# First modulation of an adaptive-norm block computed by channels, identity transposes ahead of it, and value products among the first keys

## The chip, the core and the metric

The kernel runs on one core of a Trainium2 chip. The metric is the device time of one execution in microseconds. The core's engines run side by side, each with its own queue of instructions in program order: TensorE (PE; its weight loads are listed apart as PEld), VectorE (DVE), ScalarE (ACT), GpSimd (POOL), and SyncE (SP), whose queue here issues the DMA transfers between device memory and on-chip memory. Engines wait for each other by semaphores.

## The reference

A transformer block with adaptive layer norm, in fp32: 4 batches of 512 tokens with 512 channels, 16 heads of 128, and a routed feed-forward layer of 8 experts. Cut to what matters here:

```python
mod = (_silu(L0_c) @ L0_wmod).reshape(4, 6, 1, 512)
sa, ca, ga, sb, cb, gb = (mod[:, 0], mod[:, 1], ..., mod[:, 5])
ga = (2 * (ga >= 0) - 1) * jnp.maximum(jnp.abs(ga), 0.25)      # gb likewise
h = _layernorm(x) * (1 + ca) + sa
x = x + ga * attention(h, Wq, bq, Wk, bk, Wv, bv, Wo, bo)      # causal, 16 heads
h = _layernorm(x) * (1 + cb) + sb
x = x + gb * ffn(h, ...)                                       # 2 of 8 experts, and shared ones
```

`sa` and `ca` are the shift and the scale of the first norm: 512 numbers for each of the 4 batches, from a 4x512 condition and 512x512 weights each. The change concerns how these two are made, and the order of the work around them.

## The kernel before

The order of the instructions on TensorE, VectorE, ScalarE and SP is written out by hand (`tc.manual_schedule`): each queue holds its instructions in the order in which the Python program creates them. GpSimd's queue keeps program order too. Generators split long pieces into steps, and `weave` places so many steps of one piece between so many of another.

**The opening.** SP issues the loads: the condition, the first batch's x (1 MB), the weights of the shift section `SA` (`wm`, 1 MB) and of the scale section `CA` (`wm2`, 1 MB), four small ones, and the first weights for keys, queries and values (`wk_t`, `wq_t`, `wv_t`; 512 KB each for `wk` and `wq`, 1 MB for `wv`). Each weight load is followed in `load_quadrants` by four additions on GpSimd (`sums_of_a`, lines 507 to 510). ScalarE makes `cs = silu(c)`.

- `modulation(sec, wm)`, line 169: `cs` is the small operand held in the array (4 columns), the 512 columns of the weights stream past it, four times for the four blocks of 128 inputs. The result is a 4x512 row in a bank of PSUM.
- `normed(0, 1)`: the layer norm's statistics and normalization of x, on VectorE.
- `modulate(sec, pm)`: VectorE copies the row (line 179) or adds one to it (line 177); for `SA` and `CA`, TensorE turns it by four small transposes (line 191), so that channels lie on partitions, and VectorE copies that into `mod` (line 194). For the other four sections the row is stored by a DMA.
- `quadrants(0)`: for each of four blocks of 128 channels, TensorE turns x (line 285), and ScalarE (even blocks, line 298) or VectorE (odd blocks, line 300) multiplies by the scale and adds the shift, into `h7`. Two buffers of PSUM alternate, so the third block's transposes wait for the first block's reader. Then `sums_of_b` makes three more sums and one in place on VectorE (lines 514 to 517): products are done in seven instead of eight quadrant products, and the sums are operands of them.
- `next_k(0, 0)`: seven products for the first two heads' keys, in the order 1, 2, 6, 7, 5, 4, 3 (`seven`). Products 1 and 2 read quadrants 0 and 2 of `h7`; 6, 7, 5 and 4 read the sums 5 and 4, the changed 1 and the sum 6; 3 reads quadrant 3. Each product has a buffer of PSUM out of three in rotation (tag `w`), freed by its readers on VectorE or ScalarE. Product 7's result goes through ScalarE to an addition on GpSimd (line 679), which the reader of product 4 on VectorE waits for.

**The query stretch.** `queries(0)` is 8 times seven products, 56 steps. Among them `weave` places 18 steps of `by_turns(next_v(0), rest_of_modulation())`: the seven value products (line 708) and the remaining four modulation sections, `GA`, `SB`, `CB`, `GB`, whose weights come one after the other into one buffer. For `GA` and `GB` VectorE makes six passes (lines 182 to 187). After this stretch come the attention of 16 heads with the other keys, values and output products woven in, the other batches, and the feed-forward layer.

Of the kernel before, what the change touches and what calls it, by code (L numbers as in the profile page):

```python
# [14 lines left out]
P = 128  # L15
B, S, D = 4, 512, 512
H, DH = 16, 128
NE, F, NSH = 8, 352, 2
NC = D // P
# [18 lines left out]
CAP = B * S  # L38
NT = TOPK * B * S // P + NE - 1
NA = NT - 3  # L40
NFILL = 15
NROW = NE * CAP + (NE - 1) * P
I32 = mybir.dt.int32
# [3 lines left out]
SA, CA, GA, SB, CB, GB = range(6)  # L47
# [3 lines left out]
def adaln_block_kernel(  # L51
# [18 lines left out]
    nc = tc.nc  # L70
# [10 lines left out]
    def bank(tag, name):  # L81
        if tag in ("ps", "pt"):
            return psum.tile([P, 512], F32, tag=tag, name=name)
        bufs = {"w": 3, "po": 1}[tag]
        return psum2.tile([P, 512], F32, tag=tag, bufs=bufs, name=name)

    ident = const.tile([P, P], F32, name="ident")
# [8 lines left out]
        out=before,  # L96
        in_=ones,
        compare_op=ALU.is_gt,
        fill=0.0,
# [31 lines left out]
    mod = const.tile([P, 2, NC, B], F32, name="mod")  # L131
# [23 lines left out]
    mod_rows = dram.tile([6, B, D], F32, name="mod_rows")  # L155
    cs = small.tile([P, NC, B], F32, tag="cs", bufs=1, name="cs")
# [9 lines left out]
    def modulation(sec, wm):  # L166
        pm = bank("ps", f"pm_{sec}")[:B, :]
        for c in range(NC):
            nc.tensor.matmul(
                pm, lhsT=cs[:, c, :], rhs=wm[:, c, :], start=(c == 0), stop=(c == NC - 1)  # L170
            )
        return pm

    def modulate(sec, pm):
        row = work.tile([B, D], F32, tag="gy", name=f"row_{sec}")
        if sec in (CA, CB):
            nc.vector.tensor_scalar_add(row, pm, 1.0)
        elif sec in (SA, SB):
            nc.vector.tensor_copy(row, pm)
        else:  # L180
            sgn = work.tile([B, D], F32, tag="gy", name=f"sgn_{sec}")
            nc.vector.tensor_scalar(sgn, pm, 0.0, 2.0, op0=ALU.is_ge, op1=ALU.mult)
            nc.vector.tensor_scalar_mul(row, pm, -1.0)
            nc.vector.tensor_max(row, row, pm)
            nc.vector.tensor_scalar_max(row, row, 0.25)
            nc.vector.tensor_scalar_add(sgn, sgn, -1.0)
            nc.vector.tensor_mul(row, row, sgn)
        if sec in (SA, CA):
            pt = bank("w", f"pmt_{sec}")
            for c in range(NC):  # L190
                nc.tensor.transpose(
                    pt[:, c * B : (c + 1) * B], row[:, c * P : (c + 1) * P], ident[:B, :B]
                )
            nc.vector.tensor_copy(
                mod[:, sec].rearrange("p c b -> p (c b)"), pt[:, : NC * B]
            )
        else:
            nc.sync.dma_start(out=mod_rows[sec], in_=row)

    def spread(dst, sec, b=None):  # L200

# [80 lines left out]
    def turned_block(b, n, xh, c):  # L282
        pt = bank("pt", f"pln_{n}_{b}_{c}")
        for t in range(NTB):
            nc.tensor.transpose(
                pt[:, t * P : (t + 1) * P], xh[:, t, c * P : (c + 1) * P], ident
            )
        return pt
# [223 lines left out]
    def sums_of_b(eng, w):  # L512

        eng.tensor_sub(w[:, 4], w[:, 3], w[:, 1])
        eng.tensor_add(w[:, 5], w[:, 4], w[:, 0])  # L515
        eng.tensor_sub(w[:, 1], w[:, 1], w[:, 0])
        eng.tensor_sub(w[:, 6], w[:, 5], w[:, 2])
# [76 lines left out]
    def load_wk(b, i):  # L594
        return load_quadrants("wk", wk, i, b)

    def load_wv(b, g):
        return load_quadrants("wv", wv, g, b, n=4 * DH, bufs=1)
# [257 lines left out]
    h7, late = {}, {}  # L856
# [28 lines left out]
    wm = load_wmod(att, "v", SA)  # L885
    wm2 = load_wmod(att, "wo", CA)
    for dst, src in ((bqT, bq), (bkT, bk), (bvT, bv), (gwT, router)):
        nc.sync.dma_start(out=dst, in_=src)
    wk_t = [load_wk(0, 0), load_wk(0, 1)]
    wq_t = [load_wq(0, 0), load_wq(0, 1)]  # L890
    wv_t = [load_wv(0, 0)]

    def quadrants(b, turned=()):
        h7[b] = att.tile([P, 7, 2, HW], F32, tag="h7", bufs=1, name=f"h7_{b}")
        for c in range(NC):
            turn(b, c, late["first"], h7[b], turned[c] if c < len(turned) else None)
            if c == NC - 1:
                sums_of_b(nc.vector, h7[b])
            else:
                yield  # L900

    NGB = B * NG
    kTs, vs, oSs, wos, qTs = {}, {}, {}, {}, {}

    def next_k(G, q):

        b, g = divmod(G, NG)
        kTs[G, q] = att.tile(
            [P, 2, S], F32, tag=f"kT{q}", bufs=2 - q, name=f"kT_{b}_{g}_{q}"
        )  # L910
        i = 2 * G + q
        w = wk_t.pop(0)
        save_sums("wk", i, b, w)
        yield from project_k(b, 2 * g + q, w, kTs[G, q])
        if i + 2 < 2 * NGB:
            wk_t.append(load_wk(*divmod(i + 2, H // 2)))
# [11 lines left out]
    def queries(b):  # L928
        return in_order(*(next_q(b, j) for j in range(H // 2)))

    def next_v(G):
        b, g = divmod(G, NG)
        vs[G] = att.tile([P, NTB, GH * DH], F32, tag="v", bufs=1, name=f"v_{G}")
        w = wv_t.pop(0)
        save_sums("wv", g, b, w)
        yield from project_v(b, g, w, vs[G])
        if G + 1 < NGB:
            wv_t.append(load_wv(*divmod(G + 1, NG)))
# [58 lines left out]
    def by_turns(*gens):  # L997

        gens = list(gens)
        while gens:  # L1000
            for gen in list(gens):
                if next(gen, gens) is gens:
                    gens.remove(gen)
                yield
# [13 lines left out]
    def weave(main, n, fill, count):  # L1018

        done = 0  # L1020
        for k in range(n):
            next(main, None)
            while done * n < count * (k + 1):
                done += 1
                next(fill, None)
# [11 lines left out]
    def drain(gen):  # L1037
        for _ in gen:
            pass

    SEVEN = 7

    def rest_of_modulation():
        secs = (GA, SB, CB, GB)
        wm = load_wmod(work, "xh", secs[0])
        for k, sec in enumerate(secs):
            yield
            yield
            modulate(sec, modulation(sec, wm))
            if k + 1 < len(secs):  # L1050
                wm = load_wmod(work, "xh", secs[k + 1])
# [22 lines left out]
    LAST = PLANS[:3] + [(0,) * 8]  # L1074

    with tc.manual_schedule(engines={ENG.PE, ENG.DVE, ENG.Activation, ENG.SP}):
        nc.scalar.activation(cs, cT, AF.Silu)
        load_lnexp()
        norm = normed(0, 1)
        pms = {SA: modulation(SA, wm), CA: modulation(CA, wm2)}  # L1080
        drain(norm)
        turned = [turned_block(0, 1, late[0], c) for c in range(2)]
        for sec in (SA, CA):
            modulate(sec, pms[sec])
        nc.vector.tensor_scalar_mul(sbk, bkT, qscale)
        nc.vector.tensor_sub(dbk, sbk[:, 1:H:2], sbk[:, 0:H:2])
        nc.vector.tensor_sub(dbq, bqT[:, H // 2 :], bqT[:, : H // 2])
        drain(quadrants(0, turned))
        drain(next_k(0, 0))
        fill = by_turns(next_v(0), rest_of_modulation())  # L1090
        weave(queries(0), 8 * SEVEN, fill, 18)
        drain(fill)

        pending, prepare = None, shared_sums()
        for G in range(NGB):
            b, g = divmod(G, NG)

            if G == 0:
                plans, fill = FIRST, in_order(next_k(G, 1), next_k(G + 1, 0))
            elif g == 0:  # L1100
                plans = OPENING
                fill = in_order(next_o(G - 1), next_k(G, 1), next_k(G + 1, 0))
            elif G == NGB - 1:
                plans, fill = LAST, in_order(next_k(G, 1), next_v(G), next_o(G - 1))
            else:
                plans = PLANS
                fill = in_order(
                    next_k(G, 1), next_v(G), next_o(G - 1), next_k(G + 1, 0)
                )
            for u in range(GH):  # L1110
# [25 lines left out]
                if (G, u) == (NGB - 1, 1):  # L1136
# [10 lines left out]
                        out=wst.rearrange("p c n -> p (c n)"),  # L1147
                        in_=wshr[:, NSC * SQ : NSC * SQ + NC * P],
# [21 lines left out]
                if G == 1 and u == 0:  # L1170
                    nc.sync.dma_start(
                        out=ys[NA * P :, :].rearrange("(p n) (c w) -> p (n c) w", p=P, w=P),
                        in_=nothing.unsqueeze(1).to_broadcast([P, (NT - NA) * NC, P]),
                    )

                k, n = GH * G + u - 1, NROW // P // NFILL
                if 0 <= k < NFILL:
                    nc.sync.dma_start(
                        out=xs[k * n * P : (k + 1) * n * P, :].rearrange(
                            "(p n) (c w) -> p (n c) w", p=P, w=P  # L1180
                        ),
                        in_=nothing.unsqueeze(1).to_broadcast([P, n * NC, P]),
# [253 lines left out]
    def other(i):  # L1436

        if i < 2 or i >= NA:
            return {}
# [146 lines left out]
    with tc.manual_schedule(engines={ENG.PE, ENG.DVE, ENG.Activation, ENG.SP}):  # L1586
# [39 lines left out]
        main, fill = shared(0), slots_found()  # L1626
# [15 lines left out]
        turned = {0: tile_in(0, xts.pop(0))}  # L1642
# [64 lines left out]
        main, fill = shared(2), combined()  # L1707
# [119 lines left out]
```

## Time and profile before

Three runs took 1762.41, 1763.12 and 1766.95 us; the median is 1763.12. The profiled execution took 1764.14 us, of which the span from the first to the last instruction is 1762.4.

| what | us |
|---|---|
| first matmul starts (waits for the shift section's weights) | 9.70 |
| x of the first batch in, statistics begin | 6.92 |
| scale and shift by channels both in `mod` | 22.35 |
| last block of the first norm turned | 25.82 |
| last of the four sums on VectorE ends | 32.33 |
| GpSimd through with the first loads' additions | 31.78 |
| first query product starts | 35.42 |
| first attention scores start | 115.59 |
| span ends | 1762.4 |

The DMA engines are busy from about 2 to 21 us with the opening's loads at close to 400 GB/s, and then idle until 36. In the timeline, each row gives the start and duration in microseconds, engine, line, operation, destination and sources, shapes, how many instructions are merged, and in brackets the idle time before it with what ended it. Rows of stages give for each engine the busy time and (in brackets) the number of instructions, in the order PE, PEld, DVE, ACT, POOL, then the granted clock of TensorE, the share of the DMA engines that was busy, and GB/s.

### The profile page before, as it was taken

What the parts mean: (1) busy time and instruction counts of PE and PEld (TensorE: products, weight loads), DVE (VectorE), ACT (ScalarE), POOL (GpSimd) and SP (SyncE); (2) the same over time, 40 slices, a digit from 0 to 9 for tenths busy, and PEclk for the clock granted to TensorE, in tenths of its full rate; (3) what the DMA queues carried; (4) which work ended last, traced back from release to release, by engine and by line L of the source; (5) the groups of instructions that cost most, each with busy time, mean ns of one, the idle gap of its engine ahead of it and who ended that gap; (6) DMA issues with size and microseconds to landing.
All of it is one profiled execution on the core that took longest, in us unless ns stands there. A gap on an engine that the chain in (4) does not pass through costs nothing. (4 is left out here: it accounts for less than half of the span.)

```text
span 1762.4 us, 21698 instructions
## 1 busy us (share of the span) xinstructions
PE 1701.7 (97%) x7550; PEld 1302.2 (74%) x7550; DVE 896.5 (51%) x1891; ACT 528.5 (30%) x1298; POOL 589.5 (33%) x703
## 2 busy tenths in 40 slices
PE   6999999999999999999999989999999999999998
PEld 4767787787778888688788867787788565655687
DVE  4454454546545455754655475444776232121298
ACT  1025444303453420444441144444320111111120
POOL 6335553314354220525330255533620111000370
PEclk9999999999999999999999999999999999999999
DMA  5569989736343254334324275615324555565352
GB/s 219 184 213 303 281 291 301 261 116 239 94 166 112 84 168 146 124 108 142 110 101 146 96 253 180 196 55 227 126 94 169 215 191 170 193 215 186 110 182 68
DMA packets 158526, 301.14 MB, mean 171 GB/s; under 512 B 19136, under 2 KB 99008, under 8 KB 151760
## 3 DMA queue, kind: packets, MB, share of 16 engines
q1 hardware_dynamic: 153296, 282.96, 47.7%
q0 software_dynamic: 5120, 16.78, 2.9%
q8 instruction: 61, 1.00, 0.2%
q14 instruction: 49, 0.40, 0.1%
HBM read 247.25 MB, written 97.03 MB: 195 GB/s over the span
## 5 line engine op out<-in xcount | busy, mean ns | idle before, releaser
L808 ACT ACTIVATE prob<-ps,nmax 128x128 f32<-128x128 f32 (+3 forms) x256 | 134.4, 525 | 363.2 <-DVE nmax L806 355.6
L660 PE MATMUL w_k<-h,wk 128*128 128x256 f32 x896 | 223.5, 387 | 4.6 <-DVE h L515 2.4
L745 PE MATMUL w_o<-wo,oS 128*128 128x256 f32 x896 | 208.9, 379 | 0.0
L708 PE MATMUL w_v<-wv,h 128*128 128x256 f32 x896 | 206.0, 379 | 1.3 <-DVE u_q L642 1.3
L622 PE MATMUL w_q<-h,wq 128*128 128x256 f32 x896 | 201.9, 380 | 1.8 <-DVE qT L648 1.8
L622 PEld LDWEIGHTS w_q<-h,wq 128*128 128x128 f32 x896 | 168.7, 190 | 27.8 <-issue 3.4
L660 PEld LDWEIGHTS w_k<-h,wk 128*128 128x128 f32 x896 | 165.9, 195 | 27.9 <-ACT p_k L672 5.3
L708 PEld LDWEIGHTS w_v<-wv,h 128*128 128x128 f32 x896 | 167.4, 190 | 22.9 <-DVE u_q L642 1.7
L745 PEld LDWEIGHTS w_o<-wo,oS 128*128 128x128 f32 x896 | 164.6, 190 | 21.3 <-issue 1.4
L797 PE MATMUL ps<-kT,qT 128*128 128x128 f32 (+3 forms) x512 | 173.2, 440 | 1.4 <-ACT prob L808 1.4
L839 PE MATMUL po<-probT,v 128*128 128x512 f32 (+3 forms) x512 | 150.4, 435 | 12.3 <-DVE probT L833 12.3
L839 PEld LDWEIGHTS po<-probT,v 128*128 128x128 f32 x512 | 95.5, 190 | 68.7 <-issue 30.3
L815 ACT ACTIVATE prob<-prob,rsum 128x128 f32<-128x128 f32 (+3 forms) x256 | 122.8, 551 | 63.2 <-DVE rsum L812 61.5
L825 PEld LDWEIGHTS ppt<-ident,prob 128*128 128x128 f32 x640 | 83.3, 143 | 73.4 <-issue 34.7
L758 POOL TENSOR_TENSOR xres<-xres,p_o 128x512 f32<-128x512 f32 x48 | 61.4, 1281 | 209.4 <-DVE xres L758 118.1
L806 DVE TENSOR_REDUCE nmax<-ps 128x1 f32<-128x128 f32 (+3 forms) x256 | 125.7, 491 | 8.8
L1259 PE MATMUL w_s<-h2s,ws 128*128 128x256 f32 x560 | 124.4, 381 | 3.3 <-DVE hid L1245 1.8
L1259 PEld LDWEIGHTS w_s<-h2s,ws 128*128 128x128 f32 x560 | 105.0, 190 | 20.8 <-issue 2.7
L825 PE MATMUL ppt<-ident,prob 128*128 128x128 f32 x640 | 108.4, 278 | 7.6 <-ACT prob L815 5.1
L804 DVE TENSOR_TENSOR ps<-ps,cmask 128x128 f32<-128x128 f32 x256 | 75.1, 293 | 60.4 <-PE ps L797 52.2
L1516 PE MATMUL pyt<-wdn,hTt 128*128 128x512 f32 (+1 forms) x216 | 98.7, 593 | 0.0
L1499 DVE TENSOR_TENSOR ht<-tsg,put 128x352 f32<-128x352 f32 x36 | 18.8, 521 | 147.5 <-PE put L1489 123.0
(281 smaller groups left out, 2348.9 us busy)
## 6 DMA issues: line engine op xcount, KB each, us to landing
wgu<-in_wexp_dram SPq DMA_DIRECT2D x36, 1408.0 KB
xs<-nothing SPq DMA_DIRECT2D x15, 2304.0 KB
wdn<-in_wexp_dram SPq DMA_DIRECT2D x36, 768.0 KB
wo<-sums_o SPq DMA_DIRECT2D x12, 1536.0 KB
wq<-sums_q SPq DMA_DIRECT2D x24, 640.0 KB
wk<-sums_k SPq DMA_DIRECT2D x24, 640.0 KB
wv<-sums_v SPq DMA_DIRECT2D x12, 1280.0 KB
xt<-xs SPq DMA_DIRECT2D x36, 256.0 KB
```

Source lines behind the costliest of these rows:

```text
L622: nc.tensor.matmul(dst, lhsT=w[:, sa, c, :], rhs=h7[b][:, sb_, c, :], start=c == 0, stop=c == 1,)
L660: nc.tensor.matmul(dst, lhsT=w[:, sa, c, :], rhs=h7[b][:, sb_, c, :], start=c == 0, stop=c == 1,)
L708: nc.tensor.matmul(dst[:, t2 * HW : (t2 + 1) * HW], lhsT=h7[b][:, sb_, c, t2 * P : (t2 + 1) * P], rhs=w[:, sa, c, :], start=t2 == 0 and c ...
L745: nc.tensor.matmul(dst[:, t2 * HW : (t2 + 1) * HW], lhsT=oSs[hp][:, sa, t2 * P : (t2 + 1) * P], rhs=w[:, hp, sb_, :], start=t2 == 0 and hp ...
L797: nc.tensor.matmul(ps[:, :n], lhsT=qT[:, q0 : q0 + P], rhs=kT[:, u % 2, :n], start=True, stop=True,)
L806: nc.vector.tensor_reduce(nmax, ps[:, :n], AX.X, ALU.max, negate=True)
L808: nc.scalar.activation(blk, ps[:, :n], AF.Exp, bias=nmax, accum_out=rsum[:, i : i + 1])
L815: nc.scalar.mul(blk, blk, rsum[:, k : k + 1])
L825: nc.tensor.transpose(pt[:, at : at + P], prob[:, QO[i] + j * P : QO[i] + (j + 1) * P], ident,)
L839: nc.tensor.matmul(po[:, j * P :], lhsT=v()[:, j, u * DH : (u + 1) * DH], rhs=probT[:, KO[j] : KO[j] + (NTB - j) * P], start=(j == 0), sto ...
L1259: nc.tensor.matmul(dst[:, n * HW : (n + 1) * HW], lhsT=ws[k][:, sa, c, :], rhs=h2s[b + n][:, sb_, c, :], start=(n == 0 and c == 0), stop=( ...
L1516: nc.tensor.matmul(py, lhsT=hT_t[:fn, k, :], rhs=wdn[i % 2][:fn, k * D : (k + 1) * D], start=(k == 0), stop=(k == len(FCH) - 1),)
```

## The change

Four edits.

1. `modulation_by_channels` takes the place of `modulation` and `modulate` for `SA` and `CA`. The weights are now what is held in the array, 128x128 at a time, and the 4 columns of `cs` stream past: 16 products a section, whose result has channels on partitions at once. One pass of VectorE moves it into `mod`.
2. `NIDLE = 48` transposes of the identity by itself are placed at the head of TensorE's queue; nothing reads their result.
3. The opening's order: statistics, shift section, transposes of two blocks, scale section, then `quadrants(0)` directly. The three passes that prepare biases (`sbk`, `dbk`, `dbq`) move behind it.
4. The four sums of the first batch are written out between the first products, and the first two value products are issued behind the first two key products. To that end the loads' order becomes keys, values, queries, queries, second keys; the query stretch has 16 filling steps left instead of 18.

```diff
+NIDLE = 48
...
+    def modulation_by_channels(sec, wm):
+        pm = bank("ps", f"pmt_{sec}")[:, : NC * B]
+        for k in range(NC):
+            for c in range(NC):
+                nc.tensor.matmul(
+                    pm[:, k * B : (k + 1) * B],
+                    lhsT=wm[:, c, k * P : (k + 1) * P],
+                    rhs=cs[:, c, :],
+                    start=(k == 0 and c == 0),
+                    stop=(k == NC - 1 and c == NC - 1),
+                )
+        dst = mod[:, sec].rearrange("p c b -> p (c b)")
+        if sec == CA:
+            nc.vector.tensor_scalar_add(dst, pm, 1.0)
+        else:
+            nc.vector.tensor_copy(dst, pm)
...
     def modulate(sec, pm):
...
-        if sec in (SA, CA):
-            pt = bank("w", f"pmt_{sec}")
-            for c in range(NC):
-                nc.tensor.transpose(
-                    pt[:, c * B : (c + 1) * B], row[:, c * P : (c + 1) * P], ident[:B, :B]
-                )
-            nc.vector.tensor_copy(
-                mod[:, sec].rearrange("p c b -> p (c b)"), pt[:, : NC * B]
-            )
-        else:
-            nc.sync.dma_start(out=mod_rows[sec], in_=row)
+        nc.sync.dma_start(out=mod_rows[sec], in_=row)
...
-    wk_t = [load_wk(0, 0), load_wk(0, 1)]
-    wq_t = [load_wq(0, 0), load_wq(0, 1)]
+    wk_t = [load_wk(0, 0)]
     wv_t = [load_wv(0, 0)]
+    wq_t = [load_wq(0, 0), load_wq(0, 1)]
+    wk_t.append(load_wk(0, 1))
...
     def quadrants(b, turned=()):
...
+        if b == 0:
+            return
+        sums_of_b(nc.vector, h7[b])
...
+        idle = bank("po", "idle")[:, :P]
+        for _ in range(NIDLE):
+            nc.tensor.transpose(idle, ident, ident)
         nc.scalar.activation(cs, cT, AF.Silu)
         load_lnexp()
         norm = normed(0, 1)
-        pms = {SA: modulation(SA, wm), CA: modulation(CA, wm2)}
         drain(norm)
+        modulation_by_channels(SA, wm)
         turned = [turned_block(0, 1, late[0], c) for c in range(2)]
-        for sec in (SA, CA):
-            modulate(sec, pms[sec])
+        modulation_by_channels(CA, wm2)
+        drain(quadrants(0, turned))
         nc.vector.tensor_scalar_mul(sbk, bkT, qscale)
+        keys, values, h = next_k(0, 0), next_v(0), h7[0]
+        next(keys)
+        nc.vector.tensor_sub(h[:, 4], h[:, 3], h[:, 1])
+        nc.vector.tensor_add(h[:, 5], h[:, 4], h[:, 0])
+        next(keys)
+        next(values)
+        nc.vector.tensor_sub(h[:, 1], h[:, 1], h[:, 0])
+        nc.vector.tensor_sub(h[:, 6], h[:, 5], h[:, 2])
         nc.vector.tensor_sub(dbk, sbk[:, 1:H:2], sbk[:, 0:H:2])
         nc.vector.tensor_sub(dbq, bqT[:, H // 2 :], bqT[:, : H // 2])
-        drain(quadrants(0, turned))
-        drain(next_k(0, 0))
-        fill = by_turns(next_v(0), rest_of_modulation())
-        weave(queries(0), 8 * SEVEN, fill, 18)
+        next(values)
+        drain(keys)
+        fill = by_turns(values, rest_of_modulation())
+        weave(queries(0), 8 * SEVEN, fill, 16)
         drain(fill)
```

More of the change, by code (lines that the diff above doesn't have):

```diff
@@ L172, in modulation @@
         return pm
+    def modulation_by_channels(sec, wm):
[14 more added lines that the diff above has]
+            nc.vector.tensor_copy(dst, pm)
     def modulate(sec, pm):
         row = work.tile([B, D], F32, tag="gy", name=f"row_{sec}")
-        if sec in (CA, CB):
+        if sec == CB:
             nc.vector.tensor_scalar_add(row, pm, 1.0)
-        elif sec in (SA, SB):
+        elif sec == SB:
             nc.vector.tensor_copy(row, pm)
@@ L888, in adaln_block_kernel @@
         nc.sync.dma_start(out=dst, in_=src)
-    wk_t = [load_wk(0, 0), load_wk(0, 1)]
+    wk_t = [load_wk(0, 0)]
+    wv_t = [load_wv(0, 0)]
     wq_t = [load_wq(0, 0), load_wq(0, 1)]
-    wv_t = [load_wv(0, 0)]
+    wk_t.append(load_wk(0, 1))
     def quadrants(b, turned=()):
@@ L896, in quadrants @@
             turn(b, c, late["first"], h7[b], turned[c] if c < len(turned) else None)
-            if c == NC - 1:
-                sums_of_b(nc.vector, h7[b])
-            else:
+            if c < NC - 1:
                 yield
+        if b == 0:
+            return
+        sums_of_b(nc.vector, h7[b])
     NGB = B * NG
```

## The prediction, made before the changed kernel was run

> **What bounds the kernel now.** I read the page from the top: the engines' shares, then the span in 40 slices.
>
> ```profile
> PE 1701.7 (97%) x7550; PEld 1302.2 (74%) x7550; DVE 896.5 (51%) x1891; ACT 528.5 (30%) x1298; POOL 589.5 (33%) x703
> PE   6999999999999999999999989999999999999998
> ```
>
> TensorE is busy in 97% of the span and only the first slice (44 us) falls below 8 tenths. Its idle time is 60.7 us, and the table of stages puts 9.7 us of it before the first matmul (9.70) and 4.8 us between that and 35.42, where the first query product starts. From 35.42 to 120 it idles 4.2 us. So the start is a chain of waits, and what follows is a TensorE queue: if the start ends earlier, all that follows moves. The change touches the start, so I read its timeline (start, duration, engine, line, operation):
>
> ```profile
> 9.70 9.83 PE L169 MATMUL pm<-wm,cs 128*4 128x512 f32 x16 [9.70 <-DMA wm<-in_wmod_dram]
> 19.46 1.09 PE L285 MATMUL pln<-ident,xh 128*128 128x128 f32 x8
> 21.02 0.67 DVE L177 TENSOR_SCALAR row<-pm 4x512 f32<-4x512 f32 x1
> 22.18 0.17 DVE L194 COPY mod<-pmt 128x16 f32<-128x16 f32 x1 [0.50 <-PE pmt L191]
> ...
> 25.93 1.39 DVE L514 TENSOR_TENSOR h<-h 128x512 f32<-128x512 f32 x1
> 27.36 1.63 DVE L515 TENSOR_TENSOR h<-h 128x512 f32<-128x512 f32 x1
> ...
> 29.14 6.44 PE L660 MATMUL w_k<-h,wk 128*128 128x256 f32 x20 [2.44 <-DVE h L515]
> 30.07 1.71 POOL L510 TENSOR_TENSOR wv<-wv 128x512 f32<-128x512 f32 x1
> 30.58 1.75 DVE L517 TENSOR_TENSOR h<-h 128x512 f32<-128x512 f32 x1
> ...
> 32.26 0.41 DVE L675 SCALAR_TENSOR_TENSOR kT<-w_k,p_k 128x256 f32<-128x256 f32 x1
> ```
>
> To be seen: the modulation's matmuls wait for their weights until 9.70 and take until 19.4; its scale reaches the channels at 22.35, through a row, four transposes and a copy on VectorE, twice; VectorE's four sums of the norm's blocks end at 32.33; and the second key product's sum (32.26 to 32.67) stands behind all four. The fifth key product needs its buffer, so it starts at 32.7, and the keys end at 35.42.
>
> **TensorE's clock.** Rows of stages with the granted clock (the column after the engines):
>
> ```profile
> 22.20:25.61 3.41, 1.92 (x12) 1.64 (x13) 2.56 (x6) 1.56 (x2) 3.33 (x6) 1.00 0.00 0
> 25.61:29.03 3.42, 1.09 (x6) 0.61 (x4) 3.27 (x4) 0.47 (x1) 3.34 (x3) 1.00 0.00 0
> 29.03:32.44 3.41, 3.30 (x8) 2.52 (x8) 3.41 (x3) 0.00 (x0) 2.75 (x2) 0.50 0.00 0
> 1035.95:1039.37 3.42, 1.70 (x10) 1.12 (x10) 3.32 (x7) 0.93 (x4) 2.79 (x3) 1.00 0.57 204
> 1039.37:1042.78 3.41, 3.41 (x10) 2.42 (x10) 1.41 (x4) 1.96 (x7) 3.33 (x6) 0.50 0.47 156
> ```
>
> The clock halves for whole stretches of 3.41 us on one grid (29.03, 1032.54 and 1039.37 are all steps of it). It halves after a stretch with 1.70 us of TensorE work or less and stays after one with 1.92. The first modulation matmuls are slow too, though the record says 1.00: weight loads come every 0.85 us from 10.51, and every 0.43 from 15.50.
>
> **The change, part by part.**
>
> *48 turns of the identity.* It is ready at 1.5 us. Full speed is 0.107 us a turn (the eight transposes' weight loads: 0.85 us), half speed 0.213. Half speed lasts for the rest of a stretch and one full stretch, 3.4 to 6.8 us, so they end at 1.6 + 3.4 + 32 x 0.107 = 8.4 to 1.6 + 6.8 + 16 x 0.107 = 10.1. Weights land at 9.66; nothing else is queued on TensorE. Here a rule speaks against the change: the Trainium skill, "TensorE: Matmul & The Clock Gate", Part 4, says of transposes that the full clock "doesn't engage for transpose-mode (it doesn't count as PE-busy the same way)". By that rule the 48 end at 1.6 + 10.2 = 11.8, 2.1 us after the weights, and warm nothing. The rows above disagree: of the 1.92 us in 22.20 to 25.61, 1.29 are transposes, and without them 0.63 would be less than the 1.70 that lost the clock. I take the row; the rule stays as a rival.
>
> *Modulation by channels.* Removed: two row passes (0.68, 0.67), 8 transposes, two copies, and 16 streams of 512 columns (9.8 us, 6.9 had they been at 0.43). Added: 16 products a section, each two instructions as all fp32 products here, with 128x128 weights for 4 columns. The nearest row is the router's, 8 such instructions with 8 columns:
>
> ```profile
> 449.12 0.96 PE L323 MATMUL prt<-gwT,hT 128*128 128x8 f32 x8
> 449.93 1.10 PE L797 MATMUL ps<-kT,qT 128*128 128x512 f32 x2
> ```
>
> They occupy 449.12 to 449.93: 0.102 us each, so 32 take 3.3 us. Shift section 9.70 to 13.0; two blocks' transposes (x is normed by 12.85) 0.86, to 13.85; scale section to 17.15 (its weights: the queue's next issue at 12.5 waited for them); 0.25 until VectorE sees it, 0.17 for its pass: **the scale is there at 17.55 instead of 22.35.** Nothing shows whether weight loads with 4 columns hold the clock. Bounds: 0.102 and, at half clock, 0.204. I take 0.102, as the router's row was measured at full clock; the other end is a rival.
>
> *Norm, sums and first products.* ScalarE and VectorE turn two blocks at once (0.8 each; before, three bias passes, 22.27 to 23.47, stood ahead of VectorE's): 17.6 to 18.4; two blocks transposed (0.66 and 0.44 more), the last turned by 20.35. The bias pass of 0.45, then the sums from 20.85 instead of 25.93. They are slow beside GpSimd: line 515 takes 0.69 in the other three batches and 1.63 here, alternating with GpSimd's wv additions (1.6 a pair). The changed order puts wv's additions second, until about 22.4, and the smaller ones (0.72) after. So 1.6 for the first sum and 0.6 + 0.7 = 1.3 for the others: 22.4, 23.7, key sum 24.1, 25.4, 26.7, then bias differences (0.8), value sum (0.7) 28.2, next key sum 28.6. TensorE meanwhile: keys 1 and 2 to 21.3, values 1 and 2 (1.73 each, wv lands about 16.7, behind wk at 14.0) to 24.7, keys 6 and 7 to 26.5; key 5 needs the buffer that the value sum frees: 28.2, keys done 30.8, query 1 to 31.7.
>
> *GpSimd's queue.* The second key weights' additions are now last of the loads', and the keys' own GpSimd sum (line 679) stands behind them. GpSimd has been solid from 14.09: 16 small additions at 0.69 and 4 of 1.27 are 16.2, plus some 2.1 for turns lost to VectorE: 32.4 (it was 31.78). Then 0.72 for that sum and 0.42 for VectorE's key sum, which frees the buffer of the next value product: this starts at 33.5, ends at 35.2. **That wait takes the place of the one removed**; without it the product would start at 31.7.
>
> Compare equal work. At 35.2 the keys, query 1 and three value products are done. Before: 35.42 + 0.86 + 3 x 1.73 = 41.4. **Gain 6.2 us.**
>
> *The query stretch.* Fill steps now come every 3.5 main steps (56/16; it was 56/18). Gates' six VectorE passes (58.14 to 61.7) stop TensorE for 1.29 and 1.81 us; in the new order the blocking reader is the second behind them, not the first: +0.45 and +0.3. The last weights' wait (1.14: landing 5.4 after issue) recurs twice, seven products (6.0) against 1.1 + 5.4 = 6.5: 2 x 0.5, -0.1. Together **+0.7**. On SP the store of wv's sums moves ahead of the next key load, but that load waits for the keys' last product anyway: nothing.
>
> Sum: -6.2 + 0.7 = -5.5. The profiled execution took 1764.1 (span 1762.4): 1758.6. The shown runs' median lies 1.0 lower; I take half of that: **1758.1**.
>
> **Rivals.**
>
> 1. *More.* GpSimd is through at 31.2 (pairs cost it less), and the query stretch loses nothing: 1764.1 - 7.2 = 1757, on the same half 1756.5. For it: bounds of +0.7 to nothing. Against it: solid GpSimd rows.
> 2. *Half the warmth.* Either the turns don't warm (end 11.8, shift section 5.8 us, scale at 22.1), or the small products let the clock fall (one stretch at half rate: scale at about 20, four early products half slow). Both leave the value products in the old hole, 3.5, less the query stretch: -2.9, **1761**. For it: the cited rule; small products are nearly all weight loads. Against it: the 1.92 row.
> 3. *Slower: cold array throughout the opening.* Neither turns nor small products count. Turns end at 11.8, sections take 6.5 each, the transposes 1.7: scale at 26.8, +4.4; blocks 0.9 slower; the first four products another 2.6 at half clock, while the sums run free of GpSimd by then. The value product that ended at 41.4 ends at 45.9, with the query stretch +5.2: **1769.3**. It decides if the first full clock comes after 15 us.
>
> **How the numbers follow.** Forecast 0.52, more 0.19, half 0.17, slower 0.12. Range: the forecast's own is 1756.5 to 1760 (GpSimd 1 us either way, query stretch 0.7); with rivals 1 and 2 it becomes 1755.5 to 1765, and leaves out the slower one. This kernel tells 0.3%, 5.3 us, from no change, nearly the forecast itself; its own spread falls 0.31 beyond, 0.21 within. Faster 0.31 + 0.19 = 0.50; same 0.21 + 0.17 = 0.38; slower 0.12.
>
> **What would show it.** The first modulation product at 9.7 with instructions every 0.10 us; channel scale before 18; sums from about 21, at 1.3 for the last three; GpSimd's line 679 sum beginning at 32 or later with TensorE idle before the third value product; clock of 1.00 until 30. Wrong, if small products come every 0.2 us, the first wait on TensorE is not the weights, or the stretch from 42 to 116 grows by over 2 us.

## The result, and the profile after

The changed kernel is slower. Nine runs took 1768.37 to 1772.94 us, median 1770.36; nine runs of the kernel before, on the same chip, 1761.06 to 1766.95, median 1762.54. The ratio is 1.0045, with a 95% interval of 1.0036 to 1.0053. The forecast was 1758.1, and its range ended at 1765.

The profiled execution took 1770.12 us, its span is 1767.2, against 1764.14 and 1762.4 before. From the page of the changed kernel, the busy time of the engines and TensorE's row of slices:

```profile
PE 1711.9 (97%) x7638; PEld 1320.8 (75%) x7638; DVE 893.8 (51%) x1889; ACT 527.6 (30%) x1298; POOL 587.6 (33%) x703
PE   9999999999999999899999999999899999999998
```

The first slice rose from 6 to 9 tenths, as was meant. The 24th, which had 8, has 9 now, and the 17th has 8 instead: such digits flip at nine tenths, and the two cancel. The 29th (about 1237 to 1281 us) fell to 8 without a counterpart. It is far from the opening, and there the time was lost. To find it I laid the starts of the same work side by side:

| start of | before, us | after, us | difference |
|---|---|---|---|
| first attention scores | 115.59 | 111.50 | -4.1 |
| last output product of the attention | 1240.4 | 1236.0 | -4.4 |
| first product with the shared experts' sums (tile `pst`) | 1240.6 | 1245.0 | +4.4 |
| first product of the routed experts' gates (tile `pgt`) | 1354.2 | 1360.9 | +6.7 |
| last product of all | 1757.2 | 1762.0 | +4.8 |

So in these two profiles the opening did gain, by 4.1 us, and the gain was kept for 1100 us. Then 8.8 us go between two neighbouring pieces of work, and 2.3 more just behind. TensorE's waits in the changed kernel (what waited, for what, us in total, times, longest) have a row that the kernel before has not:

```profile
PE pst L1254 <- DMA h2s<-h: 8.6, 1, 8.6
```

`h2s` is the second norm's result, which the feed-forward layer reads back from device memory. In the timeline of the kernel before, its load is issued on SP at 1221.13, 19.5 us ahead of its first reader:

```profile
1219.78 1.02 PE L797 MATMUL ps<-kT,qT 128*128 128x512 f32 x2
...
1221.13 0.96 SPq L1205 DMA_DIRECT2D h2s<-h  x2
...
1240.64 7.03 PE L1231 MATMUL pst<-h2s,wst 128*128 128x512 f32 x16
```

In the changed kernel it is issued at 1240.12, behind the last additions of the last output product:

```profile
1238.84 1.26 POOL L766 TENSOR_TENSOR xres<-xres,u_o 128x512 f32<-128x512 f32 x1
1240.12 0.80 SPq L1228 DMA_DIRECT2D h2s<-h  x2
...
1245.04 9.54 PE L1254 MATMUL pst<-h2s,wst 128*128 128x512 f32 x16 [8.64 <-DMA h2s<-h]
```

And the waits of SP's queue say what this one transfer stood for (a row each for what came last):

```profile
SPq L1228 <- DVE u_o L787: 15.4, 1, 15.4
SPq L1228 <- POOL xres L766: 6.5, 1, 6.5
SPq L1228 <- ACT p_o L788: 1.6, 1, 1.6
```

All three waits are for work on the output product's temporaries (`p_o` and `u_o` are written on ScalarE and VectorE, and GpSimd's addition into `xres` reads them). As data these have nothing to do with `h2s`. A load that waits for tiles it doesn't use waits for their place. The addresses in the built programs, in bytes of a partition, show the overlap:

```
                        before and e1_place       after and e2_before_moved
h2s_0                       93248 .. 107584         93248 .. 107584
p1, u2, u3, p5 (512 wide)  133184 .. 141376        100416 .. 108608
qT                          100416 .. 133184        108608 .. 141376
```

The pool gives places by the first appearance of a name. Before, `qT` (opened by `queries(0)`) appeared ahead of the four 512-wide temporaries of value and output products. In the changed kernel `next_v(0)` starts first, so the temporaries took the place under the later `h2s_0`. The last reader of `qT`, the scores shown above, ends at 1220.80, just ahead of the load at 1221.13; the temporaries are in use until the last output product.

The price is the idle time, 8.64 us, and a halved clock behind it. A row of stages of the changed kernel shows the clock (PE, PEld, DVE, ACT, POOL, then the granted clock):

```profile
1245.00:1248.00 3.00, 2.96 (x4) 1.44 (x5) 0.59 (x1) 0.00 (x0) 2.84 (x3) 0.50 1.07 456
```

The 16 products that took 7.03 us took 9.54, 2.5 more. Together that is 11.1 us.

**The opening after**, from the timeline (TensorE, VectorE and GpSimd rows that answer to those shown of before):

```profile
1.56 8.34 PE L1090 MATMUL idle<-ident 128*128 128x128 f32 x48 [1.56 <-POOL ident masks.py:199]
...
10.20 3.71 PE L179 MATMUL pmt<-cs,wm 128*128 128x4 f32 x32 [0.30 <-DMA wm<-in_wmod_dram]
...
13.76 1.42 PE L293 MATMUL pln<-ident,xh 128*128 128x128 f32 x8
...
14.98 6.83 PE L179 MATMUL pmt<-cs,wm 128*128 128x4 f32 x32
...
21.84 0.17 DVE L188 TENSOR_SCALAR mod<-pmt 128x16 f32<-128x16 f32 x1 [7.73 <-PE pmt L179]
...
25.91 0.68 DVE L1103 TENSOR_TENSOR h<-h 128x512 f32<-128x512 f32 x1
...
28.03 3.62 PE L716 MATMUL w_v<-wv,h 128*128 128x256 f32 x16
...
31.48 4.48 PE L668 MATMUL w_k<-h,wk 128*128 128x256 f32 x20
...
33.96 0.72 POOL L687 TENSOR_TENSOR u_k<-u_k,u_k 128x256 f32<-128x256 f32 x1 [1.33 <-ACT u_k L680]
...
36.66 1.89 PE L716 MATMUL w_v<-wv,h 128*128 128x256 f32 x8
```

The shift section took 3.71 us, the scale section, the same 32 instructions, 6.83. Why is in the rows of stages (columns as before, the clock behind the engines):

```profile
10.93:14.34 3.41, 3.41 (x32) 3.41 (x32) 2.09 (x5) 0.07 (x1) 0.00 (x0) 1.00 1.11 381
14.34:17.76 3.42, 3.42 (x19) 3.42 (x18) 0.00 (x0) 0.00 (x0) 3.15 (x5) 0.50 0.99 400
17.76:21.17 3.41, 3.41 (x17) 3.41 (x18) 0.00 (x0) 0.00 (x0) 3.33 (x4) 0.50 1.00 402
21.17:24.58 3.41, 2.33 (x11) 2.25 (x12) 0.98 (x2) 1.32 (x2) 3.33 (x6) 0.50 0.50 206
24.58:27.99 3.41, 3.41 (x10) 2.76 (x9) 2.80 (x4) 0.71 (x2) 3.33 (x5) 0.50 0.47 195
```

By the record TensorE was busy for the whole of the first stretch, with products of 4 columns for most of it, and the clock halved all the same. It stayed halved for four stretches. So the scale was in `mod` at 22.01, only 0.3 us earlier than before (22.35), and the sums begin where they did (25.91). What the opening gained is the two value products in the old hole: at 35.80 the keys are done, 0.38 later than before, but 2 x 1.73 us of value products are done as well. That is 3.1 us, and the query stretch gave 1.0 more.

### The profile page after: what moved, and what is told of

Read it like the earlier page. It is cut to its first block, busy times and chain, and to the rows that moved or that the text cites. A ratio compares the mean times of both kernels' runs of the same rounds, so it can differ in the third digit from the quotient of the medians.

```text
span 1767.2 us, 21870 instructions
## 1 busy us (share of the span) xinstructions
PE 1711.9 (97%) x7638; PEld 1320.8 (75%) x7638; DVE 893.8 (51%) x1889; ACT 527.6 (30%) x1298; POOL 587.6 (33%) x703
```

## The experiments

My theory after the result: the place of the buffers costs some 11 us, the opening is worth some 5, and the opening was held down first by the clock in the scale section. The rivals: the late load is a mere consequence of something else in the order (then claiming `qT` earlier changes nothing); or the opening gained nothing that the end can see. All ratios are against the kernel before on the same chip.

| kernel | median, us | ratio | 95% interval |
|---|---|---|---|
| after | 1770.36 | 1.0045 | 1.0036 to 1.0053 |
| e1_place | 1759.45 | 0.9971 | 0.9959 to 0.9982 |
| e2_before_moved | 1772.54 | 1.0049 | 1.0035 to 1.0062 |
| e3_wide | 1758.24 | 0.9964 | 0.9950 to 0.9977 |
| e4_no_turns | 1762.73 | 0.9994 | 0.9986 to 1.0003 |
| e5_late_wk | 1756.61 | 0.9964 | 0.9953 to 0.9975 |
| e8_bias_early | 1756.58 | 0.9961 | 0.9946 to 0.9976 |
| e6_values_only | 1759.06 | 0.9977 | 0.9969 to 0.9985 |
| e7_turns_only | 1762.34 | 0.9996 | 0.9987 to 1.0004 |
| e9_first_key | 1752.67 | 0.9946 | 0.9931 to 0.9960 |
| e10_no_turns | 1756.46 | 0.9961 | 0.9947 to 0.9974 |

The medians of the kernel before beside these were 1764.27 (e1 to e4), 1762.77 (e5 to e8) and 1763.1 (e9, e10).

### The place: given back to the changed kernel, taken from the kernel before

e1_place is the changed kernel with `qT` claimed ahead of the first value product. No instruction is changed.

```diff
+    def open_q(b):
+        qTs[b] = att.tile([P, H * S], F32, tag="qT", bufs=1, name=f"qT_{b}")
+
     def next_q(b, j):
-        if j == 0:
-            qTs[b] = att.tile([P, H * S], F32, tag="qT", bufs=1, name=f"qT_{b}")
+        if j == 0 and b not in qTs:
+            open_q(b)
...
         next(keys)
+        open_q(0)
```

> The changed kernel, with only the place of one buffer put back: the query tile is claimed before the value products claim their four temporaries, so on-chip addresses are those of before. Theory 'place': in the changed kernel the feed-forward stage's first input (h2s) lies over the temporaries of the last output product, so its load waits for that product's readers, TensorE idles 8.6 us and runs its first matmuls at half clock (9.54 instead of 7.03). Put back, both go: the load is issued near 1217, no idle before the matmuls pst, and the time falls by about 11 us, from 1770.4 to 1759 (1758 to 1761). Rival 'something else late there': the wait moves to another transfer of that stage and less than 3 us come back, 1767 to 1770.

e2_before_moved is the opposite: the kernel before, with the four temporaries claimed ahead of `qT`.

```diff
         drain(next_k(0, 0))
+        for k in ("p1", "u2", "u3", "p5"):
+            att.tile([P, S], F32, tag=f"{k}_{S}", bufs=1, name=f"{k}_held")
         fill = by_turns(next_v(0), rest_of_modulation())
```

> The kernel before, with only this changed: the four 512-wide temporaries are claimed ahead of the query tile, as the changed kernel does. No instruction is added or moved. Theory 'place': the load of h2s waits for the last output product's readers here too, TensorE idles about 8.6 us before pst and loses its clock for a stretch: 1762.5 becomes 1773 (1771 to 1775). Rival (the place does no harm without the new order of the opening): 1762 to 1764.

The load and its reader in the timeline of e1_place:

```profile
1220.99 0.90 SPq L1232 DMA_DIRECT2D h2s<-h  x2
...
1240.64 7.03 PE L1258 MATMUL pst<-h2s,wst 128*128 128x512 f32 x16
```

and of e2_before_moved:

```profile
1242.94 0.80 SPq L1207 DMA_DIRECT2D h2s<-h  x2
...
1247.93 9.31 PE L1233 MATMUL pst<-h2s,wst 128*128 128x512 f32 x16 [8.71 <-DMA h2s<-h]
```

The wait goes and comes with the place alone. e2_before_moved has the instructions of the kernel before, and is 0.49% slower, 8.6 us, where its profile has 8.71 us of idle time and 2.3 of slower products. Between e1_place and after lie 0.74%, 13 us by the ratios (10.9 by the medians, which stand beside different runs of the kernel before). The 11.1 us of the profile lie between. This is shown, and the first rival falls. So does the second: with the place put back, the change makes the kernel 0.29% faster, 5.1 us.

One caution from the same runs: e2_before_moved starts its first scores at 113.03, the kernel before at 115.59, with the same instructions up to there. The half-speed stretch of the opening lay at 23.6 to 27.0 in the one and at 29.03 to 32.44 in the other, and cut into other work. The changed kernel and e1_place, also with the same instructions, start them at 111.50 and 113.81; the profiled run of e1_place took 1762.42 us, 3.0 above its median. So totals of the opening from two single profiles can differ by some 2.5 us with the same instructions, and the gain of 4.1 us is no surer than that. The 5.1 us by the ratio rest on all runs.

### The columns: 128 instead of 4

e3_wide is e1_place with the condition repeated 32 times, so that each modulation product streams 128 columns. VectorE makes the wide operand in four copies that end at 5.0 us, while TensorE is at the turns.

```diff
-                    rhs=cs[:, c, :],
+                    rhs=late["wide"][:, c, :],
...
+        late["wide"] = work.tile([P, NC, P], F32, tag="gy", name="wide")
+        for c in range(NC):
+            nc.vector.tensor_copy(
+                late["wide"][:, c, :].rearrange("p (r b) -> p r b", b=B),
+                cs[:, c, :].unsqueeze(1).to_broadcast([P, P // B, B]),
+            )
```

> As e1_place, and the small products of the modulation stream 128 columns (the four repeated 32 times, of which only the first four are read) instead of four; four copies on VectorE before x lands make them. Theory 'columns': TensorE's clock fell at 14.3 because 4-column products, nearly all weight load, don't hold it; with 128 columns the clock stays at 1.00, the scale section takes 3.5 to 4 us instead of 6.8, the scale is there about 3 us earlier than 22.0, and the time is 2 to 4 us under e1_place, 1755 to 1757. Rival 'the gap or the transposes lost the clock': clock and time as e1_place within 1 us.

From the rows of stages of e3_wide:

```profile
14.00:18.00 4.00, 4.00 (x37) 3.89 (x35) 0.00 (x0) 0.00 (x0) 3.70 (x5) 1.00 0.99 398
```

and from its timeline:

```profile
14.35 3.74 PE L179 MATMUL pmt<-wide,wm 128*128 128x128 f32 x32
18.12 0.17 DVE L189 TENSOR_SCALAR mod<-pmt 128x16 f32<-128x16 f32 x1 [4.27 <-PE pmt L179]
...
22.09 0.68 DVE L1114 TENSOR_TENSOR h<-h 128x512 f32<-128x512 f32 x1
...
27.51 2.86 PE L669 MATMUL w_k<-h,wk 128*128 128x256 f32 x12 [0.34 <-DVE v L742]
...
32.42 0.72 POOL L688 TENSOR_TENSOR u_k<-u_k,u_k 128x256 f32<-128x256 f32 x1
33.17 0.42 DVE L684 SCALAR_TENSOR_TENSOR kT<-w_k,u_k 128x256 f32<-128x256 f32 x1 [5.39 <-POOL u_k L688]
33.65 3.56 PE L717 MATMUL w_v<-wv,h 128*128 128x256 f32 x8 [2.42 <-DVE kT L684]
```

With 32 times the columns the section takes the same 3.7 us (its pace is that of the weight loads), and the clock holds at 1.00 until 33.4 us. The scale is in `mod` at 18.29. So the number of columns, not the record's busy time, decided over the clock. But the time came down by 0.07% only, within the intervals: the third value product now stands still for 2.42 us behind VectorE's key sum (line 684), which stands behind GpSimd's (line 688). GpSimd began its sum at 32.42, and the value product started at 33.65. The prediction had put it at 33.5.

### The turns: taken away, and alone

e4_no_turns is e1_place without the 48 turns (`NIDLE = 0`).

> As e1_place, without the 48 turns of the identity. Theory 'turns warm but the warmth is lost by the scale section': the shift section starts at 9.7 to 10.2 and runs at half clock, 6.8 us instead of 3.7, so the scale comes 3 to 3.5 us later and the time is 2 to 3.5 us above e1_place, 1761 to 1763. Rival 'turns worth nothing': within 1 us of e1_place.

From its timeline:

```profile
9.94 6.96 PE L179 MATMUL pmt<-cs,wm 128*128 128x4 f32 x32 [9.94 <-DMA wm<-in_wmod_dram]
```

Its shift section took 6.96 us instead of e1_place's 5.12 (whose clock halved within it, at 11.7), VectorE's pass for the scale started at 25.36 instead of 23.28, and the ratio rose from 0.9971 to 0.9994, with intervals that don't touch: 4.1 us by the ratios, 3.3 by the medians. e7_turns_only is the kernel before with the turns and nothing else.

```diff
+NIDLE = 48
...
+        idle = bank("po", "idle")[:, :P]
+        for _ in range(NIDLE):
+            nc.tensor.transpose(idle, ident, ident)
```

> The kernel before with only the 48 turns of the identity. Theory 'turns count for the clock': the first modulation's streams of 512 columns run at full clock from the start, 8 x 0.43 = 3.4 us a section instead of 6.4 for the first, they end near 16.6 instead of 19.4, and some 2.9 us carry over: ratio 0.9984. Rival (the Trainium skill's rule that transposes don't engage the full clock): turns end near 11.8, the first section starts 2 us later and still cold, 2 us slower.

From its timeline:

```profile
1.55 7.17 PE L1080 MATMUL idle<-ident 128*128 128x128 f32 x48 [1.55 <-POOL ident masks.py:199]
9.81 7.03 PE L170 MATMUL pm<-wm,cs 128*4 128x512 f32 x16 [1.09 <-DMA wm<-in_wmod_dram]
...
32.30 0.72 POOL L680 TENSOR_TENSOR u_k<-u_k,u_k 128x256 f32<-128x256 f32 x1
...
33.54 1.99 PE L709 MATMUL w_v<-wv,h 128*128 128x256 f32 x8 [2.00 <-DVE kT L676]
```

The two modulation sections took 7.03 us instead of 9.83: turns of the identity do bring the array to full speed. At the end no gain is left that stands clear of the noise (0.9996). Part of it goes to the same gate: here too a value product then waits for GpSimd's key sum, 2.00 us. That is not all. The first scores start at 112.17, 3.4 us ahead of the kernel before, and the first product with the shared experts' sums at 1239.79, 0.9 us ahead; 2.6 us were lost between the two (see the open point below).

### The value products alone

e6_values_only is the kernel before with the loads' order, the sums written out and the value products among the first keys (and the place kept), without turns and with the old modulation.

```diff
-        drain(next_k(0, 0))
-        fill = by_turns(next_v(0), rest_of_modulation())
-        weave(queries(0), 8 * SEVEN, fill, 18)
+        keys, values, h = next_k(0, 0), next_v(0), h7[0]
+        next(keys)
+        open_q(0)
...
+        fill = by_turns(values, rest_of_modulation())
+        weave(queries(0), 8 * SEVEN, fill, 16)
```

> The kernel before with only the order of loads, sums and first value products of the change (the query tile claimed first, so that addresses stay). Theory 'hole': the two value products (3.45 us) fill the hole in which the keys wait for the sums, and the stalls of the query stretch fall by 1 us as they did in the changed kernel: 4 to 4.5 us less than before, ratio 0.9975. Rival 'the sums get later by the same amount': within 1 us of before.

Ratio 0.9977 [0.9969, 0.9985], first scores at 111.45: nearly all that the whole change has with the place put back (0.9971). In the kernel as changed, the new modulation and the turns together are worth little beside it. Without turns the new modulation is even the slower one: e4_no_turns has the same value order, with the new modulation and its place in the opening, and stands at 0.9994 [0.9986, 1.0003], 0.17% or 3 us above e6_values_only, with intervals that just don't touch. At half speed its two sections took 6.96 and 6.83 us, where the two old ones took 8.92 together. So the turns there mostly gave back what the new modulation loses without them.

### The gate on GpSimd

e5_late_wk is e3_wide with the second key weights' load, and with it its four additions, created behind the first keys' GpSimd sum in the program.

```diff
     wq_t = [load_wq(0, 0), load_wq(0, 1)]
-    wk_t.append(load_wk(0, 1))
...
         next(values)
+        for _ in range(4):
+            next(keys)
+        wk_t.append(load_wk(0, 1))
         drain(keys)
```

> As e3_wide, and the second key weights are loaded and added up behind the first keys' own three GpSimd passes instead of ahead of them. Theory 'GpSimd's queue': in e3_wide the third value product waited 2.4 us for a key sum that stood behind those additions, and ran at half clock after the gap (3.56 us instead of 1.89). Both go: no wait of w_v, and the time falls by about 4 us under e3_wide, to 1754. Rival 'VectorE's sums set the end of the keys': the product starts at most 0.5 us earlier and the time stays within 1.5 us of e3_wide.

A miss. From its timeline:

```profile
29.82 0.73 POOL L516 TENSOR_TENSOR wk<-wk 128x256 f32<-128x256 f32 x1
...
31.99 0.72 POOL L519 TENSOR_TENSOR wk<-wk 128x256 f32<-128x256 f32 x1
32.67 0.72 POOL L688 TENSOR_TENSOR u_k<-u_k,u_k 128x256 f32<-128x256 f32 x1
...
33.90 3.46 PE L717 MATMUL w_v<-wv,h 128*128 128x256 f32 x8 [2.43 <-DVE kT L684]
```

The additions (lines 516 to 519) still run ahead of the sum (line 688), which the program now creates first. So GpSimd's queue is not in program order: the order written by hand covers TensorE, VectorE, ScalarE and SP (the engines that `manual_schedule` is given), and GpSimd is not among them. What was told of its queue in the description of the kernel is wrong.

e8_bias_early, made beside it, is e5_late_wk with the three bias passes of VectorE ahead of the scale section.

```diff
         modulation_by_channels(SA, wm)
+        nc.vector.tensor_scalar_mul(sbk, bkT, qscale)
+        nc.vector.tensor_sub(dbk, sbk[:, 1:H:2], sbk[:, 0:H:2])
+        nc.vector.tensor_sub(dbq, bqT[:, H // 2 :], bqT[:, : H // 2])
```

> As e5_late_wk, and the three bias passes (1.15, 0.68 and 0.15 us in e3_wide) are put where VectorE waits for the scale section. Theory 'TensorE sets the opening by now': its queue had only 0.5 us of slack left before the fifth key product, so 0.5 us less than e5_late_wk. Rival 'VectorE still does': 1.9 us less.

The fifth key product lost its wait (20 key instructions in one row from 25.37), the wait of the value product grew from 2.43 to 2.96 us, and the time stayed (0.9961 beside 0.9964). The passes were covered by the GpSimd gate, as the modulation had been.

e9_first_key takes the gate away: the first key's three additions run on VectorE.

```diff
+        eng = nc.vector if (b, i) == (0, 0) else nc.gpsimd
...
-            nc.gpsimd.tensor_add(o, o, u)
+            eng.tensor_add(o, o, u)
...
-                "22": lambda p5, u3: nc.gpsimd.tensor_add(out(1, 1), p5, u3),
+                "22": lambda p5, u3: eng.tensor_add(out(1, 1), p5, u3),
...
-                "u4": lambda o, p5, u2: nc.gpsimd.tensor_add(o, p5, u2),
+                "u4": lambda o, p5, u2: eng.tensor_add(o, p5, u2),
```

> As e8_bias_early, and the first key's three GpSimd additions are done on VectorE. In e5_late_wk and e8_bias_early the wait stayed (2.4 and 3.0 us): the four additions of the second key weights still ran ahead of them on GpSimd, whose order the program's order doesn't set. Theory 'GpSimd's queue': on VectorE the key sum is there before 30, the third value product starts by 31 instead of 33.7 and at full clock (1.89 instead of 3.35): 3 to 4 us less than e8_bias_early, first attention scores before 108.5, ratio 0.994. Rival 'the gain of the opening is given back in the attention stretch': the scores come earlier, and the time stays within 1.5 us of e8_bias_early.

From its timeline:

```profile
25.36 4.48 PE L669 MATMUL w_k<-h,wk 128*128 128x256 f32 x20
29.68 1.03 PE L631 MATMUL w_q<-h,wq 128*128 128x256 f32 x4
30.74 1.97 PE L719 MATMUL w_v<-wv,h 128*128 128x256 f32 x8
```

None of these rows has a wait in brackets, the value product starts 3.2 us earlier than in e5_late_wk, and the first scores start at 105.9 (111.3 in e8_bias_early). The clock stays at 1.00 past them, where in e3_wide the gap was followed by half speed from 33.4 on (3.56 us for the value product, here 1.97). Its ratio of 0.9946 is 9.5 us below the kernel before, and by the two ratios 1.0%, some 17 us, below the changed kernel: it beats both. Its interval still overlaps that of e8_bias_early (0.9961 [0.9946, 0.9976]); that the wait went is sure from the trace, how much of the total it was worth is less so. e10_no_turns is e9_first_key without the turns.

> As e9_first_key, without the 48 turns. Theory 'turns keep their worth once the rest can use it': the shift section at half clock costs up to 3.2 us and the clock comes up only after 13 to 16: 3 to 4 us above e9_first_key. Rival 'worth nothing': within 1 us.

The shift section takes 6.66 us instead of 3.81, the first scores start at 108.29, and the median rises by 3.8 us; the intervals of the two ratios overlap, so the size is less sure than the sign that the trace shows.

## Why the prediction was wrong

**The step that failed** is in the first part: "So the start is a chain of waits, and what follows is a TensorE queue: if the start ends earlier, all that follows moves." It looked for effects of the change only where instructions were moved. But moving `next_v(0)` ahead of `queries(0)` also moved the first appearance of five buffers, and with it their places, and at 1240 us a load came to wait for the buffers it now overlaps. That is 11.1 us on a forecast gain of 5.5. None of the rivals had such a step; the one on the slow side was the cold array, and the array was warm at 10 us. Nothing in the trace of before tells of it directly. What could have told is that the load of `h2s` is issued at 1221, with no wait on SP that the profile shows and 19.5 us ahead of its reader: a cover of that size on a load depends on its place being free.

Without that, the total was near: -0.29% [-0.41, -0.18], 5.1 us against 5.5. Its steps were less good than its sum: some were too high and some too low, so that the nearness is in part luck.

- **The 48 turns: right.** Ended between 8.4 and 10.1 by the forecast, at 9.90 here and at 8.72 in e7_turns_only. The row was right against the rule of the Trainium skill ("TensorE: Matmul & The Clock Gate", Part 4) that transposes don't engage the full clock: by it the turns would have taken 10.2 us, they took 8.34 and 7.17, and in e7_turns_only, where TensorE had done nothing but the turns by then, the modulation behind them took 7.03 us instead of 9.83.
- **The shift section: right**, 3.71 us for 32 instructions, 0.116 us each against 0.102, 0.5 us later at the start.
- **The scale section: wrong.** "I take 0.102, as the router's row was measured at full clock; the other end is a rival." It took 0.213 an instruction: the other end. The router's eight instructions are 0.8 us in a stretch of other work, and say what one costs at full clock, not whether they hold it. The mechanism was named in the rival "half the warmth". Scale at 22.01 instead of 17.55, keys done at 35.8 instead of 30.8.
- **The sums: over-priced.** 1.6 and three of 1.3 by the forecast; 0.68, 1.10, 0.89 and 1.21 measured. They ran beside GpSimd's 256-wide additions, not the 512-wide ones.
- **GpSimd's gate: right in e3_wide and covered here.** With the clock held, the value product started at 33.65 (33.5 by the forecast), waiting on the key sum as said. In the changed kernel GpSimd itself waits for ScalarE at 33.96, so the late keys hid it.
- **Equal work: 6.2 by the forecast, 3.1 measured.** The late scale is the larger part, and the cheaper sums made up for some of it.
- **The query stretch: +0.7 by the forecast, -1.0 measured.** The gates' passes stopped TensorE for 3.1 us in two waits, the same sum as before (1.29 and 1.81), so the +0.75 did not come; and the wait of 1.14 for the last weights went altogether, where 0.1 was taken off. This offset part of the scale's error.
- **The profiled run against the median.** Half of 1.0 us was taken; the profiled run before lay 1.6 above the median of its nine. It decides nothing.

Open: in the profiles of single runs, the gains of the opening shrink between the first scores and 1240 us in some kernels (1125.0 us from one to the other before, 1127.4 in e5_late_wk, 1124.0 in e9_first_key). The clock has a part in it: the half-speed stretches between 100 and 1240 us come to 13.7 us in the kernel before, but to 20.5 in e3_wide, e6_values_only and e7_turns_only, and in these three TensorE is busy 2.3 to 3.4 us longer over that work than before (1096.1). They are not the only cause: e5_late_wk has 13.7 too and is busy only 0.8 us longer; there the attention's products wait 13.7 us for VectorE's copies (`probT`) instead of 12.3. Why the stretches and waits fall as they do was not settled.

## What to carry to other kernels

When a change moves the first use of a buffer in a pool, compare the addresses of before and after, and look at every early load whose place overlaps something new: a prefetch far behind the change can turn into a wait. Where a stage is gated in turn by the clock, by VectorE and by GpSimd, as here, the removal of one gate pays little; name the next one, and remove them together. And ask of an engine that "goes in program order" whether the hand-written order includes it.

## What the hardware showed that was not expected

- TensorE's clock doesn't go by the record's busy time. A stretch of 3.41 us that was busy for 3.41, most of it in products of 4 columns, was followed by half speed; with 128 columns at the same pace the clock stayed at 1.00. Before, 1.92 us of wider work in a stretch had been enough to keep it. To bring it back from half speed, 2.33 us in a stretch (21.17 to 24.58 of the changed kernel, mostly transposes) were not; how much it takes was not measured.
- Turns of the identity in fp32 count as work for the clock (the 48 took 7.17 us in e7_turns_only, where half speed throughout would be 10.2; the modulation behind them took 7.03, without turns 9.83 in the kernel before and 8.92 in e6_values_only).
- The same instructions can meet the clock's grid at another phase in another run: half speed at 29.03 in the kernel before and at 23.6 in e2_before_moved, 2.6 us apart at the first scores.
